# Softmax sums of a masked attention unit: in every second grouped step, products with ones on TensorE in place of VectorE's transposing reduction

## The chip, the cores and the metric

One NeuronCore of a Trainium2 chip runs the kernel. TensorE multiplies matrices and writes to PSUM, which has 8 banks of 128 partitions by 512 fp32 numbers; VectorE, ScalarE and GpSimd are three more engines with instruction queues of their own, each worked off in order; SyncE issues DMA transfers. The metric is the device time of one execution in microseconds, as the median of several. Before the change it is 3578.74 us (three runs, 3578.55 to 3579.28).

## The reference

Four cross attentions follow one another, each with a residual, for a batch of 4 sequences of 512 rows and 256 columns against a context of 1024 rows and 512 columns. Layers 0, 2 and 3 are alike and called masked here; layer 1 is called grouped. All arithmetic is fp32. Cut to what matters:

```python
# layers 0, 2, 3 ("masked"): 16 heads of 64
q, k, v = x @ Wq, ctx @ Wk, ctx @ Wv
logits = q @ k.T / 8 + col_bias            # col_bias: -20 * (1 - mask) in at most four key columns
probs  = softmax(logits, axis=keys)        # over 1024 keys
x      = probs @ v @ Wo + bo + x
# layer 1 ("grouped"): 16 query heads of 16, 4 key heads of 16
xn    = x * rsqrt(mean(x * x) + eps) * norm_w
probs = softmax((xn @ wq) @ (ctx @ wk).T / 4)
x     = x + probs @ (ctx @ wv) @ wo
```

The part of it that the change touches is the sum over keys by which the exponentials of a masked layer are divided.

## The kernel before

**Tiling.** Everything is kept transposed: logits have the keys on partitions and the queries along the free axis. A *unit* of a masked layer is a pair of heads of one sequence: 8 tiles of 128 keys (on partitions) by 1024 columns, which are 512 queries of the one head and 512 of the other. A unit of the grouped layer is a quarter of its heads in two halves, `h` 0 and 1, again 8 tiles of 128 by 1024 each. There are 96 masked units and 32 grouped ones. One *step* works on one masked unit, and in 32 of the 96 on a grouped unit too; `order()` lays the units out by two strings of digits (`MASKED_TURNS`, `GROUPED_TURNS`), so that grouped units with `h` 0 and 1 fall on alternate steps. A product of fp32 matrices of 512 columns appears in the profile as two records.

**A masked unit.** In its own step, `scores` (L803, L809) makes the 8 logit tiles, ScalarE copies each to SBUF (L813), and VectorE keeps a running maximum (L817). `max_quarters` and `max_everywhere` reduce that maximum over partitions and spread it again (L854 to L880). VectorE subtracts it from each tile (L888), ScalarE takes the exponential (L894), and GpSimd adds the 8 exponential tiles up into one, `g.acc` (L933, seven additions). In the *next* step the unit is called `g1`: `attend` multiplies the exponentials with the values on TensorE (L833) into `g1.place`, a PSUM bank, and `normalise(g1)` works on VectorE: `reciprocal_sums` reduces `g.acc` over partitions with a transposing reduction (L854 reading `st`), adds the quarters up in small pieces (L958 to L963), takes the reciprocal (L966), spreads it by a transposition (L968), and `scale_out` multiplies the attended values by it (L979), which gives the bank of `g1.place` back. One PSUM bank serves `reciprocal_sums` as room. `project_out` (L997) takes the result through Wo a step or more later, two units at a time.

**A grouped unit** (`lam`). Its logits are made one step ahead, as `coming`, by four calls of `logits_pair` (L780), which take two double PSUM banks each and give one or both of them back when ScalarE has copied them (L786). In its own step GpSimd subtracts the maximum (L886), ScalarE takes the exponentials, `attend_grouped` multiplies with the values (L833, 32 columns wide), and `keep_even` (ScalarE, L843) and `keep_odd` (VectorE, L847) bring the halves of the result to SBUF. After the second half, `h` = 1, `turn_grouped` divides by the sum, which a column of ones in the values has made: VectorE instructions L944, L945, L946 and L950, with one PSUM bank as room.

**What sets the order.** The schedule is written out by hand in the step loop. TensorE's work between the scores and the next step is a list, `fill`, of (estimated us, function). In a step with a grouped unit of `h` = 1 it is: the output projection of two units (3.6), the projection of one or two query sets (1.7 each, L721), and the eight parts of the keys of the next two units (1.7 each, L514; two parts, `part` 0 and 1, accumulate in one bank). `attend_grouped` (3.6) is inserted where the estimates ahead of it reach 9.5:

```python
            while where < len(fill) and total < 9.5:
                total += fill[where][0]
                where += 1
            fill.insert(where, (3.6, attend_grouped))
```

As the list is gone through, a running estimate `now` decides when `events` (the subtractions and exponentials of the unit) are issued to VectorE and ScalarE, and when the four `logits_pair` calls come in between, the first at 12.0. Ahead of the first one, `behind_exponentials` issues the rest of `events` and then the list `late`: `normalise(g1)`, `keep_odd(lam)` and, where `h` = 1, `turn_grouped(lam)`, in this order on VectorE.

**PSUM banks.** `Place(width)` hands out banks at the time of building, the one given back longest ago first (a single bank whose neighbour is taken is preferred); what a bank's next user waits for on the chip follows from that choice. In the 16 steps with `h` = 1 there are three kinds. In ten the list has two query projections; in two (the second halves of the first quarter in sequences 1 and of the second quarter in sequence 3) it has one; in both kinds the four pairs of the next grouped unit follow. In four steps (each sequence's last) it has at most one and there is no next grouped unit, so no pairs.

Of the kernel before, what the change touches and what calls it, by code (L numbers as in the profile page):

```python
# [16 lines left out]
P = 128  # L17
B, S, C = 4, 512, 256
# [62 lines left out]
def kernel(ctx: ExitStack, tc: tile.TileContext, a: dict, out: bass.AP):  # L81
    nc = tc.nc
# [8 lines left out]
    def t_(shape, tag, name, bufs=1, dtype=FP):  # L91
        return sb.tile(shape, dtype, tag=tag, name=name, bufs=bufs)
# [40 lines left out]
    def give_set(g):  # L133
        sets_free.append(g.set)
# [6 lines left out]
    ones = t_([P, P], "ones", "ones")  # L141
# [595 lines left out]
    def reciprocal_rows(out_, in_, room):  # L737


        turned = room[:, 0:S]  # L740
        short = t_([P, S // 32, 1], "short", f"short{len(turns)}")
        turns.append(0)
        nc.vector.transpose(turned, in_)
        nc.vector.reciprocal(short, turned.rearrange("p (c r) -> p c r", r=32)[:, :, 0:1])
        nc.vector.transpose(
            out_.rearrange("p (c r) -> p c r", r=32), short.to_broadcast([P, S // 32, 32])
        )
# [71 lines left out]
    def place_out(g, width=1):  # L819
        g.place = Place(width)  # L820
        g.po, g.psum = g.place.ap[:, 0:S], g.place.ap[:, S:]

    def attend(g, blocks=range(NT)):
        for t in blocks:
            for j in range(2):
                rows = g.rows[j]
                if not g.masked:
                    rows = slice(64 * g.h + 32 * j, 64 * g.h + 32 * (j + 1))
                at, first, last = rows, 0, NT - 1
                if not g.masked:  # L830
                    at = slice(64 * (t % 2) + 32 * j, 64 * (t % 2) + 32 * (j + 1))
                    first, last = t % 2, NT - 2 + t % 2
                nc.tensor.matmul(  # L833
                    g.po[at, :], lhsT=g.v[:, t, rows], rhs=g.st[t][:, j * S : (j + 1) * S],
                    start=(t == first), stop=(t == last),
                )

    def keep_even(g):


        if g.h == 0:
            gq[g.b, "o"] = t_([P, S], "o1", f"o1_{g.name}")
        nc.scalar.copy(gq[g.b, "o"][64 * g.h : 64 * (g.h + 1), :], g.po[0:64, :])  # L843

    def keep_odd(g):
        half = gq[g.b, "o"][64 * g.h : 64 * (g.h + 1), :]
        nc.vector.tensor_tensor(half, half, g.po[64:128, :], ALU.add)  # L847
        g.place.back()
# [35 lines left out]
    def subtract(g, t):  # L884
        if not g.masked:
            nc.gpsimd.tensor_tensor(g.st[t], g.st[t], g.mb, ALU.subtract)  # L886
            return
        nc.vector.tensor_tensor(g.st[t], g.st[t], g.mb, ALU.subtract)  # L888
        if t == NT - 1:
            g.mb_place.back()  # L890
# [18 lines left out]
    def attend_last(g):  # L909

        place_out(g, 2)
        parts_of = [g.st[t] for t in range(g.now, NT)] + [g.acc]

        def add(n):
            for j in range(2):
                nc.tensor.matmul(
                    g.psum[g.rows[j], :], lhsT=ones[:, 0:64], rhs=parts_of[n][:, j * S : (j + 1) * S],
                    start=(n == 0), stop=(n == NT - g.now),
                )

        for t in range(NT):
            for j in range(2):
                nc.tensor.matmul(
                    g.po[g.rows[j], :], lhsT=g.v[:, t, g.rows[j]], rhs=g.st[t][:, j * S : (j + 1) * S],
                    start=(t == 0), stop=(t == NT - 1),
                )
            if t >= g.now:
                add(t - g.now)
        add(NT - g.now)
        g.ot = t_([P, S], "ot", f"ot_{g.name}", bufs=3)  # L930
# [4 lines left out]
    def turn_grouped(g):  # L935
        w = Place(1)
        normalise_grouped(g, w.ap)
        w.back()
# [33 lines left out]
    def normalise(g):  # L972
        w = Place(1)
        reciprocal_sums(g, w.ap)
        w.back()
        scale_out(g)

    def scale_out(g):
        nc.vector.tensor_tensor(g.ot, g.po, g.ot, ALU.mult)  # L979
        g.place.back()  # L980

    def project_out(*of):

        g = of[0]
        x, acc = xs[g.l, g.b], xs.get((g.l + 1, g.b))
        opens = acc is None
        if opens and g.masked:
            acc = new_state(g.l + 1, g.b)
        elif opens:

            acc = xs[g.l + 1, g.b] = x
            x_at[g.l + 1, g.b] = x_at[g.l, g.b]
        w = Place()
        m = w.ap
        for k in range(KC):
            for each in of:
                nc.tensor.matmul(  # L997
                    m[:, k * S : (k + 1) * S], lhsT=each.wo[:, k * P : (k + 1) * P], rhs=each.ot,
                    start=each is g, stop=each is of[-1],
                )  # L1000
        y = m.rearrange("p (k q) -> p k q", q=S)

        def add_last(q):
            nc.vector.tensor_tensor(acc[:, :, q], y[:, :, q], acc[:, :, q], ALU.add)

        def add():
            if g is masked[-1]:
                for i in range(0, NI, 2):
                    add_last(slice(i * P, (i + 2) * P))
                    store(g.b, range(i, i + 2))  # L1010
                left[g.b] = -1
            elif opens and g.masked:
                bo = columns[f"L{g.l}_xattn_bo"]
                for k in range(KC):
                    nc.vector.scalar_tensor_tensor(
                        acc[:, k, :], y[:, k, :], bo[:, k : k + 1], x[:, k, :], ALU.add, ALU.add
                    )
            else:
                nc.vector.tensor_tensor(acc, y, x if opens else acc, ALU.add)
            w.back()  # L1020

        left[g.b] -= len(of)
        return add
# [33 lines left out]
    def at(n):  # L1057
        return steps[n] if 0 <= n < len(steps) else (None, None)
# [8 lines left out]
    def head(g):  # L1067
        return steps[step_of[1, g.b, 0]][1]
# [28 lines left out]
    g0, g1 = masked[0:2]  # L1097
# [41 lines left out]
    for n in range(len(steps) + 2):  # L1139
        g, lam = at(n)  # L1140
        follows, coming = at(n + 1)
        soon = at(n + 2)[1]
        g1, attended = attended, g
        ending = n >= len(steps) - 2
# [61 lines left out]
        late = []  # L1206
# [23 lines left out]
        for each in (follows, coming):  # L1230
            if each and (not (each.l and each.u == 0) if each.masked else each.h == 0):
                queries.append(each)

        if lam:
            for t in range(NT):
                subtract(lam, t)
# [11 lines left out]
        if g1 and g:  # L1248
            attend(g1)
            give_set(g1)  # L1250
            if not ending:
                late.append(lambda: normalise(g1))
        elif g1:
            attend_last(g1)
            adds = [project_out(*each) for each in outs]
            outs = []
            reciprocal_rows(g1.ot, g1.psum, g1.mx)
            scale_out(g1)
            for add in adds:
                add()  # L1260
# [8 lines left out]
        if coming:  # L1269
# [6 lines left out]
        fill, of_grouped = (  # L1276
            [
                (1.8 * len(each), lambda each=each: project_out(*each))
                for each in outs if each[0].masked == m
            ]  # L1280
            for m in (True, False)
        )
        outs = []
        of_queries = [(1.7, lambda each=each: project_q(each)) for each in queries]
        if fast_k:
# [3 lines left out]
            fill = of_keys[:2] + fill + of_keys[2:4] + of_queries + of_keys[4:]  # L1289
        elif fast_v:  # L1290
            of_values = fast_values(g)
            fill = of_values[:2] + fill + of_queries + of_values[2:]
# [6 lines left out]
        if lam:  # L1299

            def attend_grouped():
                while any(of is lam for _, of, _ in events):
                    events.pop(0)[2]()
                lam.v = head(lam).v
                place_out(lam)
                attend(lam)
                give_set(lam)
                late.append(lambda: keep_odd(lam))
                if lam.h == 1:
                    late.append(lambda: turn_grouped(lam))  # L1310
                return lambda: keep_even(lam)

            total, where = 0.0, 0
            while where < len(fill) and total < 9.5:
                total += fill[where][0]
                where += 1
            fill.insert(where, (3.6, attend_grouped))
# [17 lines left out]
        if g1 and g and ending:  # L1335

            def by_products():
                sums(g1)
                return lambda: late.append(
                    lambda: (reciprocal_rows(g1.ot, g1.psum, g1.mx), scale_out(g1))  # L1340
                )

            fill.append((0.9, by_products))
# [48 lines left out]
```

## Time and profile before

| | |
|---|---|
| runs | 3578.55, 3578.74, 3579.28 us |
| profiled execution | 3578.93 us, of which the span of its instructions is 3577.2 us; mean granted TensorE clock 0.995 |
| TensorE | 3495.1 us of matrix products, 98% of the span |
| VectorE | 3045.3 us, 85% |
| GpSimd | 2495.9 us, 70% |
| ScalarE | 2352.9 us, 66% |
| steps with a grouped unit of `h` = 1 | ten of 49.64 to 51.28 us, two of 52.59 and 53.39 us, four of 39.07 to 40.13 us |
| L854 reading `st` (VectorE) | 1257 ns, 93 times |
| L958, L959, L960, L963 (four), L966, L968, L979 (VectorE) | 193, 191, 181, 165 each, 253, 711, 692 ns |
| L833, 64 columns wide (TensorE) | 32 records, that is 16 products, in 7.02 us |

Times are microseconds from the first instruction unless marked ns. PE is TensorE, PEld its weight loads, DVE VectorE, ACT ScalarE, POOL GpSimd. A line of the timeline has the start, the length from the first start to the last end, engine, source line, operation, what is written and read, sizes, and how many; in square brackets stands how long the engine had been idle and who ended that. The ends of matrix products are modelled, so lengths of a stage on TensorE are better taken from one start to the next. The granted clock is a share of full speed. The length of a step is the time from its first L803 to the next step's.

### The profile page before, as it was taken

Reading aid. Unit: us, or ns where it says so; the run is one execution under the profiler, and the core shown is the slowest. Engines: PE = TensorE matmul, PEld = TensorE weight load, DVE = VectorE, ACT = ScalarE, POOL = GpSimd, SP = SyncE. Lnnn points to the kernel's source line nnn. Section 1 sums busy time; section 2 is a strip of 40 time slices with the busy share of each in tenths; the row PEclk is TensorE's granted clock in tenths of the full one; section 3 lists DMA queues with packets and bytes.
Section 4 is the critical chain, followed back from the end, with each engine's and each line's share of the span. In section 5 each row is a group of like instructions: output and inputs, shape, how many; then the busy total and the mean of one; then the engine's idle time right before and its main releaser. Section 6 shows DMA issues by size and latency. Waiting matters only on the chain.

```text
span 3577.2 us, 42743 instructions
## 1 busy us (share of the span) xinstructions
PE 3495.1 (98%) x15390; PEld 1703.6 (48%) x15390; DVE 3045.3 (85%) x4174; ACT 2352.9 (66%) x2737; POOL 2495.9 (70%) x1273
## 2 busy tenths in 40 slices
PE   8999999999999999999999999999999999999998
PEld 4454444444444444444554545454444445454554
DVE  7878788987889978889888888888788988888887
ACT  4565577775777757777565666665577775666664
POOL 3565477774777747777678778777477776769774
PEclk9999999999999999999999999999999999999999
DMA  3222101002100020001001111010201011002110
GB/s 90 62 93 82 56 20 46 23 19 56 39 23 23 19 78 17 23 23 43 27 27 50 33 33 51 27 51 18 57 22 38 23 34 43 26 27 74 33 32 7
DMA packets 159384, 140.16 MB, mean 39 GB/s; under 512 B 42424, under 2 KB 142264, under 8 KB 158660
## 3 DMA queue, kind: packets, MB, share of 16 engines
q1 hardware_dynamic: 153518, 124.32, 11.2%
q0 software_dynamic: 2560, 8.39, 0.7%
q10 hardware_dynamic: 3094, 4.72, 0.6%
q8 instruction: 122, 2.00, 0.2%
q14 instruction: 90, 0.74, 0.1%
HBM read 122.71 MB, written 10.49 MB: 37 GB/s over the span
## 4 chain that ended last, share of the span: by engine, by line
PE 67%; DVE 23%; ACT 7%; issue 3%; POOL 1%; ACTq 0%; DMA 0%; DVEq 0%; SPq 0%; POOLq 0%
PE ps L608 13%; PE ps L803 13%; PE ps L833 13%; PE ps L514 9%; DVE ps L817 8%; PE ps L553 7%; DVE st L888 5%; ACT st L894 4%; PE ps L780 3%; PE ps L721 3%; PE ps L997 3%; DVE ps L854 2%; DVE ps L880 1%; DVE ps L792 1%; ACT st L786 1%
## 5 line engine op out<-in xcount | busy, mean ns | idle before, releaser
L933 POOL TENSOR_TENSOR st<-st 128x1024 f32<-128x1024 f32 x668 | 1581.0, 2367 | 725.6 <-ACT st L894 680.8
L894 ACT ACTIVATE st<-st 128x1024 f32<-128x1024 f32 x1024 | 1036.3, 1058 | 300.1 <-DVE st L888 233.6
L817 DVE TENSOR_TENSOR ps<-ps,st 128x1024 f32<-128x1024 f32 x672 | 828.0, 1232 | 295.7 <-ACT st L813 234.2
L888 DVE TENSOR_TENSOR st<-st,ps 128x1024 f32<-128x1024 f32 x768 | 883.5, 1216 | 3.3
L886 POOL TENSOR_TENSOR st<-st 128x1024 f32<-128x1024 f32 x256 | 596.8, 2374 | 312.4 <-DVE st L880 207.0
L833 PE MATMUL ps<-st,v 128*64 128x512 f32 (+1 forms) x4064 | 800.7, 595 | 9.0 <-ACT st L894 8.9
L813 ACT COPY st<-ps 128x1024 f32<-128x1024 f32 x768 | 716.6, 1048 | 96.5 <-PE ps L809 65.1
L803 PE MATMUL ps<-qt,kt 64*128 64x512 f32 x3072 | 719.5, 601 | 26.4 <-DVE ps L854 19.6
L833 PEld LDWEIGHTS ps<-st,v 128*64 128x64 f32 (+1 forms) x4064 | 241.4, 130 | 550.2 <-issue 435.5
L803 PEld LDWEIGHTS ps<-qt,kt 64*128 64x128 f32 x3072 | 301.9, 186 | 382.4 <-issue 131.3
L514 PE MATMUL ps<-ctx,wk 128*128 128x512 f32 x896 | 417.1, 611 | 2.2 <-ACT ctx L416 1.1
L553 PE MATMUL ps<-wv,ctx 128*128 128x256 f32 x1792 | 408.0, 382 | 0.0
L553 PEld LDWEIGHTS ps<-wv,ctx 128*128 128x128 f32 x1792 | 335.5, 190 | 102.4 <-issue 59.4
L792 DVE TENSOR_TENSOR ps<-ps,st 128x1024 f32<-128x1024 f32 x224 | 276.1, 1232 | 73.3 <-ACT st L786 60.2
L786 ACT COPY st<-ps 128x1024 f32<-128x1024 f32 x256 | 247.4, 1014 | 83.1 <-PE ps L780 80.2
L514 PEld LDWEIGHTS ps<-ctx,wk 128*128 128x128 f32 x896 | 167.3, 193 | 239.5 <-issue 215.5
L608 PE MATMUL ps<-st 128*128 128x128 f32 (+1 forms) x1200 | 229.0, 339 | 6.4 <-ACT ps L631 6.4
L623 ACT COPY st<-ps 128x512 f32<-128x512 f32 x40 | 23.4, 585 | 301.6 <-PE ps L608 301.6
L780 PE MATMUL ps<-qt,kt 32*128 32x512 f32 x1024 | 183.3, 640 | 18.0 <-DVE o L847 9.7
L608 PEld LDWEIGHTS ps<-st 128*128 128x128 f32 x1200 | 158.6, 192 | 75.1 <-issue 65.1
L721 PE MATMUL ps<-x,wq 128*128 128x512 f32 x384 | 186.2, 608 | 1.3 <-ACT x L379 1.1
L997 PE MATMUL ps<-ot,wo 128*128 128x512 f32 x384 | 175.8, 600 | 0.7 <-DVE ot L979 0.7
(177 smaller groups left out, 2833.1 us busy)
## 6 DMA issues: line engine op xcount, KB each, us to landing
ctx<-kept SPq DMA_DIRECT2D x24, 1024.0 KB
wk<-in_L_xattn_Wk_dram SPq DMA_DIRECT2D x47, 512.0 KB
wv<-in_L_xattn_Wv_dram SPq DMA_DIRECT2D x47, 512.0 KB
wq<-in_L_xattn_Wq_dram SPq DMA_DIRECT2D x96, 128.0 KB
wo<-in_L_xattn_Wo_dram SPq DMA_DIRECT2D x96, 128.0 KB
st<-kept SPq DMA_DIRECT2D x4, 2048.0 KB
kept<-st SPq DMA_DIRECT2D x12, 512.0 KB
qt<-qt ACTq DMA_DIRECT2D x32, 128.0 KB
```

Of the source, the lines that this page charges most:

```text
L514: nc.tensor.matmul(m, lhsT=g.w["k"][:, k, :], rhs=ctx_half[g.b, n][:, k, :], start=(k == 0), stop=(k == KT - 1),)
L553: nc.tensor.matmul(m[:, half * 2 * P : (half + 1) * 2 * P], lhsT=ctx_half[g.b, t // 4][:, k, t % 4 * P : (t % 4 + 1) * P], rhs=g.w["v2"][: ...
L608: nc.tensor.matmul(m if is_keys else m[:, q], lhsT=right[:, k, :] if is_keys else left_[:, k, q], rhs=left_[:, k, :] if is_keys else right ...
L792: nc.vector.tensor_tensor(top, top, g.st[t], ALU.max)
L803: nc.tensor.matmul(m[:, j * S : (j + 1) * S], lhsT=g.kt[g.rows[j], keys], rhs=g.qt[g.rows[j], :], start=True, stop=t > 0,)
L813: nc.scalar.copy(g.st[t], m)
L817: nc.vector.tensor_tensor(top, top, g.st[t], ALU.max)
L833: nc.tensor.matmul(g.po[at, :], lhsT=g.v[:, t, rows], rhs=g.st[t][:, j * S : (j + 1) * S], start=(t == first), stop=(t == last),)
L886: nc.gpsimd.tensor_tensor(g.st[t], g.st[t], g.mb, ALU.subtract)
L888: nc.vector.tensor_tensor(g.st[t], g.st[t], g.mb, ALU.subtract)
L894: nc.scalar.activation(st, st, AF.Exp)
L933: nc.gpsimd.tensor_tensor(g.acc, g.st[0] if t == 1 else g.acc, g.st[t], ALU.add)
```

## The change

In steps whose grouped unit has `h` = 1 (and that have both `g` and `g1`), `normalise(g1)` is not put on `late`. In its place a new item goes into `fill` behind the first one, with an estimate of 0.9: `sums_beside(g1)` takes a PSUM bank and issues two products of a 128 by 64 matrix of ones with the two halves of `g1.acc` on TensorE, which leave in every row of the bank the sums of the head that this row belongs to. It then puts `turned` at the front of `late`: VectorE transposes that bank into `g.ot` (L743), takes the reciprocal of one column in 32 (L744), spreads it by a second transposition (L745, which are the lines of `reciprocal_rows`), gives the bank back and does `scale_out`. The estimate of 0.9 counts in the loop that places `attend_grouped`, and in `now`.

```diff
+    def sums_beside(g):
+        w = Place(1)
+        for j in range(2):
+            nc.tensor.matmul(
+                w.ap[g.rows[j], :], lhsT=ones[:, 0:64], rhs=g.acc[:, j * S : (j + 1) * S],
+                start=True, stop=True,
+            )
+
+        def turned():
+            g.ot = t_([P, S], "ot", f"ot_{g.name}", bufs=3)
+            reciprocal_rows(g.ot, w.ap, g.ot)
+            w.back()
+            scale_out(g)
+
+        return turned
...
+        by_ones = bool(g and g1 and lam and lam.h == 1)
...
-            if not ending:
+            if not ending and not by_ones:
                 late.append(lambda: normalise(g1))
...
+            if by_ones:
+                fill.insert(1, (0.9, lambda: late.insert(0, sums_beside(g1))))
             total, where = 0.0, 0
             while where < len(fill) and total < 9.5:
```

Built, the two programs differ in the 16 steps with `h` = 1 in three ways beside the instructions exchanged:

- On TensorE `attend_grouped` stands one key part (L514, two products) earlier, and that part follows the fourth pair; without pairs it simply follows `attend_grouped`.
- On ScalarE, in the ten steps with two query projections, the grouped unit's eighth exponential keeps its place behind the same work, and the first copy of keys (L519) moves from ahead of L843 to behind the first pair's copies. In the two steps with one query projection the eighth exponential moves from behind the first L519 to ahead of it.
- PSUM banks are dealt out differently. In the ten steps the first pair's second double bank is now the one that holds `g1.place` and the sums, where it was one of a freed query bank and a freed key bank; the second pair's first double bank now holds the room of `turn_grouped`, where it was the banks of `g1.place` and of the grouped unit. In the two steps the first pair's second double bank was that of `g1.place` and of the grouped unit and is now one of freed query and key banks; the second pair's first one holds the room of `turn_grouped` in both programs.

The order in the other steps is unchanged. Lines from L979 on have numbers higher by 16 to 19 in the changed kernel.

## The prediction

> **What bounds the kernel now.** I read the page first: busy times, then the chain that ended last.
>
> ```profile
> PE 3495.1 (98%) x15390; PEld 1703.6 (48%) x15390; DVE 3045.3 (85%) x4174; ACT 2352.9 (66%) x2737; POOL 2495.9 (70%) x1273
> PE 67%; DVE 23%; ACT 7%; issue 3%; POOL 1%; ACTq 0%; DMA 0%; DVEq 0%; SPq 0%; POOLq 0%
> ```
>
> TensorE is nearly always in use, so a product added costs its time unless it falls into a wait of TensorE, and VectorE time taken away gains only where TensorE waits for it. Next the waits of TensorE over the whole run:
>
> ```profile
> PE ps L803 <- DVE ps L854: 19.6, 16, 1.8
> PE ps L780 <- DVE o L847: 9.7, 14, 1.1
> PE ps L833 <- ACT st L894: 8.9, 10, 1.2
> ```
>
> The columns after the colon are total us, times, longest. The first is in the scores, ahead of the change. The others are the attention and the pairs of grouped steps, so I read the timeline of one changed step (it starts at 583.52 and lasts 49.64 us), TensorE first, then ScalarE and VectorE:
>
> ```profile
> 603.24 1.88 PE L721 MATMUL ps<-x,wq 128*128 128x512 f32 x4
> ...
> 606.67 3.60 PE L514 MATMUL ps<-ctx,wk 128*128 128x512 f32 x8
> 610.20 3.63 PE L833 MATMUL ps<-st,v 128*32 128x512 f32 x28
> 614.61 1.05 PE L833 MATMUL ps<-st,v 128*32 128x512 f32 x4 [0.79 <-ACT st L894]
> 615.60 1.70 PE L780 MATMUL ps<-qt,kt 32*128 32x512 f32 x8
> 617.22 1.98 PE L514 MATMUL ps<-ctx,wk 128*128 128x512 f32 x4
> 619.14 2.62 PE L780 MATMUL ps<-qt,kt 32*128 32x512 f32 x8
> 621.68 1.98 PE L514 MATMUL ps<-ctx,wk 128*128 128x512 f32 x4
> ```
>
> ScalarE:
>
> ```profile
> 612.56 2.95 ACT L894 ACTIVATE st<-st 128x1024 f32<-128x1024 f32 x3 [0.55 <-DVE st L888]
> 615.53 0.58 ACT L519 COPY kt<-ps 128x512 f32<-128x512 f32 x1
> 616.01 2.01 ACT L894 ACTIVATE st<-st 128x1024 f32<-128x1024 f32 x2
> 618.05 0.58 ACT L843 COPY o<-ps 64x512 f32<-64x512 f32 x1
> ```
>
> VectorE:
>
> ```profile
> 613.06 1.26 DVE L854 TRANSPOSE_TENSOR_REDUCE ps<-st 128x32 f32<-128x1024 f32 x1
> ...
> 618.66 0.69 DVE L847 TENSOR_TENSOR o<-o,ps 64x512 f32<-64x512 f32 x1 [1.18 <-ACT o L843]
> ...
> 621.20 0.69 DVE L950 TENSOR_TENSOR o<-o,ps 128x512 f32<-128x512 f32 x1
> ```
>
> See three things. The last block of the grouped attention starts at 614.61, when its exponential (the second of the three at 612.56) ends; TensorE has been out of work since about 610.20 + 28 x 0.1115 = 613.32 (0.1115 is a record of the undisturbed attention, 32 in 3.57 us, in the step that starts at 633.16). A pair takes 1.07 us undisturbed (the third, from 623.60 to 624.67); the first takes 1.62 and the second 2.54, so they wait 0.55 and 1.47 us. And behind the chain that the change shortens VectorE stands idle for 1.18 us until ScalarE's L843. So VectorE's work there isn't on the path now.
>
> **The change part by part.** *VectorE.* Removed per step: 1257 + 193 + 191 + 181 + 4 x 165 + 253 + 711 ns, 3.45 us. Added: two transpositions and a reciprocal, 716 + 253 + 712 ns by the same lines at the kernel's end, 1.68. Its queue is 1.8 us shorter, but L847, the next on it, waits for L843: worth nothing by itself.
>
> *TensorE.* The two products are four records at 7.02 / 32 = 0.22, 0.88 us a step. Their sums have been ready since GpSimd's last addition at 580.3, 23 us before 603.2, so they add no wait there. That GpSimd's subtractions come next on its queue changes nothing.
>
> *The attention one key part earlier.* In ten steps (like this one) TensorE now arrives at 603.24 + 0.88 + 3.43 (L721) + 1.77 (one key part) = 609.32 in place of 610.20. The eighth exponential has the same work ahead of it on ScalarE, which was in arrears, so it ends at the same time and the last block starts at 614.61 as before. The products hide in that wait, and 0.88 us more of it is idle, but a key part of 1.77 us is left for later. (That key part's bank is now one of the projection's, which VectorE's L1019 frees at 607.49, while TensorE comes at 607.55; what it might lose there falls into the wait too.)
>
> *The first pair* begins at 615.60. Its second half waited for the copy L519, which is done at 616.11. It will use the banks of the sums and of the attended values, which VectorE frees at 613.06 + 0.75 + 0.29 + 0.75 + 0.69 = 615.54 (the rows with their pauses): no wait, and it ends at 616.67 rather than 617.22. The key part behind it ends at 618.59.
>
> *The second pair* is the dear one. It must now wait for the end of `turn_grouped`, L950. L843 starts 0.6 us earlier, as L519 no longer stands ahead of it, so L847 runs from about 618.06, and L950 ends 3.23 us later (618.66 to 621.89 now): 621.29. The pair runs from 621.35 to 622.42, where it was done at 621.68: 0.74 us later, after an idle time of 2.8 us. What is queued behind the waiting pair is all of TensorE's work, two more pairs and the keys.
>
> *The rest of the step* took 11.48 us and has 1.77 more, less the 0.16 that the fourth pair waited. Sum for such a step: 0.74 + 1.77 - 0.1 = 2.4 us. The next step starts later by as much, and its engines begin with what its scores bring, so nothing is made up.
>
> *Two steps* (at 938 and 2721) have one query projection. In the latter, counted from its start, the eighth exponential comes about 0.6 us sooner on ScalarE, as a copy of keys no longer precedes it, so the last block starts at 30.65 rather than 31.25 and the first pair, whose banks are free, runs from 31.63 to 32.70; a key part ends at 34.6. L843 stays behind all exponentials, so L950 still ends at 37.9 and the second pair runs from 37.95 to 39.0. Behind it come 1.92 + 1.07 + 1.92 + 1.07 + 3.53 + 1.72 + 1.81: the step ends at 52.05 in place of 52.59, -0.5 us. I take that for both. *Four steps* have no pairs and hardly wait in the attention (32 records in 3.61 us): 0.88 each. Sum: 10 x 2.4 - 2 x 0.5 + 4 x 0.88 = 26.5 us.
>
> *The clock.* What 26.5 leaves out is in this table of stretches in the step at 2721, whose pairs wait long already (length, busy times of the five engines, granted clock, DMA):
>
> ```profile
> 2753.60:2757.00 3.40, 2.47 (x8) 0.58 (x4) 2.63 (x4) 2.96 (x4) 3.32 (x2) 1.00 0.00 0
> 2757.00:2760.40 3.40, 3.40 (x6) 1.18 (x4) 2.96 (x5) 1.01 (x1) 3.24 (x3) 0.51 0.00 0
> ```
>
> After a stretch in which products were few, the clock is halved for 3.4 us, though all that time is busy; its L514 records stand 0.85 us apart in place of 0.43. That costs 1.7 us. Five stretches more are like it (near 429, 876, 975, 1392, 2634; each has a mean of 0.66 over 5 us), all behind about 1.5 to 2.5 us of idle time within some 3.5. The ten steps, with waits of 1.3 and 1.5 us that lie apart, have none. The changed step has two waits, of 2.2 us in the attention and 2.8 at the second pair. A drop after the first is nearly hidden by the second; one after the second costs 1.7 us in full. Bounds: none in any step, 0 us; one in each of the twelve, 12 x 1.7 = 20.4. I take half of the ten and both of the others, as their wait at the second pair grows to 3.3 us, at 1.5 each since part of the 3.4 us may still lie in the wait: 7 x 1.5 = 10.5. Sum 37 us.
>
> [...]
>
> The profiled execution took 3578.93 us, its span and 1.7, against a median of 3578.74: both give 3616 with 37 added.
>
> **The rivals.**
> *No drop of the clock:* all of the above without 10.5. Speaks for it: no drop in the ten steps now. Against: the longer waits. 3578.7 + 26.5 = 3605.
> *A drop in every step with pairs:* 26.5 + 20.4 gives 3626.
> *Not slower: the second pair doesn't wait for L950.* The place is the bank that the pair takes. Were it free, the pair would start on arrival at 618.59, 2.8 us earlier, and a step of the ten would end 0.3 us sooner than now; with 3.5 for the four and -1 for the two that is 3578, no change. It decides at a wait under 0.4 us. Against it: the profile shows pairs of the step at 2721 held by L979 and L847 through their banks, and L950 stands on the same queue behind them.
> *A gain from VectorE's 1.8 us:* it would need VectorE, not ScalarE's L843, to be late for the pairs; the 1.18 us idle ahead of L847 says no. At most the second pair's 1.47 us in ten steps less 3.5: 3567.
> *The sums wait for GpSimd:* each us would cost ten to sixteen; 23 us of margin speak against it.
>
> **How the numbers follow.** Forecast 3616 (some drops) 0.45; no drop, 3605, 0.25; drops everywhere, 3626 or somewhat above, 0.18; mis-sized second wait between 3587 and 3600, 0.05; not slower 0.05; gain 0.02. The range runs from the no-drop case less 6 us to the all-drops case with 4 more: 3599 to 3630. A measurement of this kernel tells about 0.2% (7 us) from no change: slower 0.93, same 0.05, faster 0.02.
>
> **What would show it.** In the changed kernel: four new records near 20 us into each of the 16 steps without idle time ahead; the last attention block still about 31.1 us in; a second pair that starts near 37.8 us and waits for L950; ten steps near 52.0 us, or 53.7 with a stretch at half clock; four near 39.95. It is wrong if ScalarE's exponentials move, if the pairs' banks are freed sooner than I have it, or if the next step makes the time up.

## The result, and the profile after

The changed kernel takes 3619.24 us (median of four runs, 3618.18 to 3621.81) against 3579.01 for the kernel before beside it (3578.55 to 3579.94): a ratio of 1.0114 with a 95% interval of 1.0101 to 1.0126, slower by 40 us. The profiled execution took 3619.03 us, its span is 3617.3 us and its mean granted clock 0.992.

The page after, busy times and the chain that ended last:

```profile
PE 3504.4 (97%) x15454; PEld 1697.4 (47%) x15454; DVE 3017.1 (83%) x4062; ACT 2350.3 (65%) x2737; POOL 2495.3 (69%) x1273
PE 67%; DVE 23%; ACT 6%; issue 2%; ACTq 0%; DVEq 0%; DMA 0%; POOL 0%; POOLq 0%
```

VectorE has lost 28 us of work and TensorE has gained 9, which explains neither the direction nor the size. The waits of TensorE over the whole run do (total us, times, longest):

```profile
PE ps L780 <- DVE o L950: 29.2, 12, 2.7
PE ps L803 <- DVE ps L854: 19.2, 16, 1.8
PE ps L833 <- ACT st L894: 13.4, 11, 1.3
PE ps L780 <- DVE o L847: 9.2, 14, 0.7
```

The first line is new: a pair of the coming grouped unit waits for L950, the end of the turn in place, once in each of the twelve steps that have pairs. The scores' wait (second line) is as before, the grouped attention's (third) went from 8.9 to 13.4 us.

The step that the prediction followed now starts at 585.77. Its timeline, TensorE:

```profile
605.59 1.08 PE L981 MATMUL ps<-st,ones 128*64 128x512 f32 x4
606.60 1.98 PE L721 MATMUL ps<-x,wq 128*128 128x512 f32 x4
...
610.13 1.88 PE L514 MATMUL ps<-ctx,wk 128*128 128x512 f32 x4
611.94 3.63 PE L833 MATMUL ps<-st,v 128*32 128x512 f32 x28
616.88 1.05 PE L833 MATMUL ps<-st,v 128*32 128x512 f32 x4 [1.31 <-ACT st L894]
617.86 1.14 PE L780 MATMUL ps<-qt,kt 32*128 32x512 f32 x8
618.93 1.98 PE L514 MATMUL ps<-ctx,wk 128*128 128x512 f32 x4
623.59 2.09 PE L780 MATMUL ps<-qt,kt 32*128 32x512 f32 x8 [2.67 <-DVE o L950]
625.61 2.56 PE L514 MATMUL ps<-ctx,wk 128*128 128x512 f32 x4
```

VectorE in the same step:

```profile
620.30 0.69 DVE L847 TENSOR_TENSOR o<-o,ps 64x512 f32<-64x512 f32 x1 [2.52 <-ACT o L843]
...
622.85 0.69 DVE L950 TENSOR_TENSOR o<-o,ps 128x512 f32<-128x512 f32 x1
```

Read it from the top. The two products start at 605.59, with no idle time ahead of them. The attention comes 1.77 us of work earlier and finds the eighth exponential unfinished, so its last block starts at 616.88, 31.11 us into the step, where it also started before. The first pair no longer waits. The second one does, for 2.67 us, until L950 is done. VectorE's queue is shorter by 1.8 us, and most of that is now idle time ahead of L847 (2.52 us until ScalarE's L843, where it was 1.18). The pair and the key part behind it are then slow (2.02 us to the next start in place of 1.07, a length of 2.56 in place of 1.98). The stretches around them show why (from and to, length, busy times of the five engines with the number of instructions, granted clock, DMA):

```profile
616.56:619.97 3.41, 3.09 (x15) 1.01 (x16) 1.19 (x2) 3.38 (x5) 3.33 (x2) 1.00 0.01 2
619.97:623.39 3.42, 0.95 (x3) 0.12 (x1) 2.95 (x5) 2.72 (x4) 3.26 (x3) 1.00 0.00 0
623.39:626.80 3.41, 3.21 (x10) 1.19 (x11) 1.33 (x3) 1.09 (x2) 3.33 (x2) 0.50 0.00 0
```

In the second stretch TensorE was busy for 0.95 us of 3.42; in the third it has half clock. Such a stretch at half clock is called a drop here.

Step by step, from one first L803 to the next: the ten steps with two query projections are 2.43 us longer where the clock did not drop (three of them) and 3.6 to 4.2 us longer where it did (seven). Together that is 35.2 us. The two steps with one projection together add 0.9, the four without pairs 4.6, and all other steps take back 0.5. The sum is 40.1 us, the difference of the two profiled executions.

### The profile page after: what moved, and what is told of

It reads as the page before. It is cut to its first block, busy times and chain, and to the rows that moved or that the text cites. A ratio compares the mean times of both kernels' runs of the same rounds, so it can differ in the third digit from the quotient of the medians.

```text
span 3617.3 us, 42774 instructions
## 1 busy us (share of the span) xinstructions
PE 3504.4 (97%) x15454; PEld 1697.4 (47%) x15454; DVE 3017.1 (83%) x4062; ACT 2350.3 (65%) x2737; POOL 2495.3 (69%) x1273
## 4 chain that ended last, share of the span: by engine, by line
PE 67%; DVE 23%; ACT 6%; issue 2%; ACTq 0%; DVEq 0%; DMA 0%; POOL 0%; POOLq 0%
PE ps L608 13%; PE ps L803 13%; PE ps L833 12%; PE ps L514 9%; DVE ps L817 8%; PE ps L553 7%; DVE st L888 5%; ACT st L894 4%; PE ps L780 4%; PE ps L721 3%; PE ps L1013 3%; DVE ps L854 2%; DVE ps L880 1%; DVE ps L792 1%; DVE every L869 1%
## 5 line engine op out<-in xcount | busy, mean ns | idle before, releaser
L833 PE MATMUL ps<-st,v 128*64 128x512 f32 (+1 forms) x4064 | 802.2, 595 | 14.1 <-ACT st L894 13.4
L803 PE MATMUL ps<-qt,kt 64*128 64x512 f32 x3072 | 716.6, 599 | 25.3 <-DVE ps L854 19.2
L803 PEld LDWEIGHTS ps<-qt,kt 64*128 64x128 f32 x3072 | 298.4, 186 | 381.4 <-ACT st L813 134.2
L514 PE MATMUL ps<-ctx,wk 128*128 128x512 f32 x896 | 424.1, 619 | 2.2 <-ACT ctx L416 2.2
L792 DVE TENSOR_TENSOR ps<-ps,st 128x1024 f32<-128x1024 f32 x224 | 276.1, 1233 | 97.2 <-ACT st L786 86.8
L514 PEld LDWEIGHTS ps<-ctx,wk 128*128 128x128 f32 x896 | 169.3, 196 | 245.3 <-issue 225.3
L780 PE MATMUL ps<-qt,kt 32*128 32x512 f32 x1024 | 167.2, 654 | 44.3 <-DVE o L950 29.2
L721 PE MATMUL ps<-x,wq 128*128 128x512 f32 x384 | 187.5, 611 | 1.7 <-ACT x L379 1.1
L1013 PE MATMUL ps<-ot,wo 128*128 128x512 f32 x384 | 175.8, 600 | 0.7 <-DVE ot L995 0.7
```

The source lines that it names most:

```text
L514: nc.tensor.matmul(m, lhsT=g.w["k"][:, k, :], rhs=ctx_half[g.b, n][:, k, :], start=(k == 0), stop=(k == KT - 1),)
L792: nc.vector.tensor_tensor(top, top, g.st[t], ALU.max)
L803: nc.tensor.matmul(m[:, j * S : (j + 1) * S], lhsT=g.kt[g.rows[j], keys], rhs=g.qt[g.rows[j], :], start=True, stop=t > 0,)
L833: nc.tensor.matmul(g.po[at, :], lhsT=g.v[:, t, rows], rhs=g.st[t][:, j * S : (j + 1) * S], start=(t == first), stop=(t == last),)
```

## The experiments

Each ran beside the kernel before on the same chip. The columns "ten", "two", "four" and "rest" give by how many us the steps of each kind, together, were longer in the profiled execution than in that of before; "rest" is all other steps and the ends.

| run | median us | ratio to before, 95% interval | ten | two | four | rest |
|---|---|---|---|---|---|---|
| changed kernel | 3619.2 | 1.0114 [1.0101, 1.0126] | +35.2 | +0.9 | +4.6 | -0.5 |
| attention at its old place | 3588.0 | 1.0025 [1.0015, 1.0035] | +6.1 | +0.5 | +4.4 | -1.7 |
| early place alone | 3637.7 | 1.0163 [1.0149, 1.0177] | +48.8 | +2.3 | +5.0 | +2.4 |
| products alone | 3589.5 | 1.0027 [1.0017, 1.0038] | +7.0 | +1.6 | +6.2 | -1.4 |
| VectorE's path alone | 3576.4 | 0.9991 [0.9982, 1.0000] | +0.2 | +2.9 | -0.3 | -3.1 |
| wait filled, two products | 3606.3 | 1.0073 [1.0060, 1.0087] | +23.7 | -0.8 | +4.6 | +0.3 |
| wait filled, one product | 3606.7 | 1.0078 [1.0064, 1.0091] | +23.7 | -0.8 | +4.6 | +0.2 |
| room given back late | 3611.4 | 1.0085 [1.0071, 1.0099] | +20.4 | +2.7 | +4.6 | +4.7 |
| attention one part later | 3607.8 | 1.0079 [1.0065, 1.0093] | -3.9 | -4.4 | +4.1 | +32.1 |
| put together | 3579.3 | 1.0000 [0.9991, 1.0009] | -0.7 | -4.9 | 0.0 | +5.9 |
| put together, second | 3573.6 | 0.9983 [0.9974, 0.9992] | +1.6 | -4.5 | -0.3 | -1.8 |
| before, room late | 3581.0 | 1.0005 [0.9996, 1.0014] | 0.0 | -0.3 | 0.0 | +0.6 |

The theory: the loss comes from the place of the attention, which the 0.9 in the list moves one key part ahead. That leaves the key part for later, deals out the banks so that the second pair waits for L950, and the wait brings the clock down. The rivals: the products cost their own time, VectorE's new path delays something, or the clock drops for another reason.

### Attention at its old place

```diff
-                fill.insert(1, (0.9, lambda: late.insert(0, sums_beside(g1))))
+                fill.insert(1, (0.0, lambda: late.insert(0, sums_beside(g1))))
```

> The changed kernel, with the estimate of the sums in the list of fillers set from 0.9 to 0.0, so that the grouped attention stays behind as many key parts as before; the products and VectorE's shorter path stay. Theory (the loss is the attention's place: the key part left for later and, through the banks, the second pair's wait for L950): in the ten steps the second pair takes a double bank without the turn's room, so they return to within 0.3 us of the kernel before, the products hidden in the attention's wait; the four steps without pairs keep their +0.9 to +1.25 us, of which most comes back in the step behind; no more than one or two drops of the clock beyond the six of before. Time 3579 to 3586, that is 33 to 40 us under the changed kernel. Rival (the products themselves cost about 1.2 us in each of 16 steps): about 3598.

Measured: 3588.0 us, 31 us under the changed kernel and 2 above the range given. The ten steps are back: five are within 0.02 us of before and one 0.45 shorter. Four have a drop and are 1.5 to 1.7 us longer. The wait for L950 is left in the two steps alone:

```profile
PE ps L803 <- DVE ps L854: 19.2, 16, 1.8
PE ps L780 <- DVE o L847: 8.9, 12, 0.7
...
PE ps L780 <- DVE o L950: 5.3, 2, 2.7
```

The theory holds, and the products, which are all in this kernel, cost nothing in the ten steps. The estimate also counts in `now`, so the edit takes back, with the place, the new order on ScalarE (L519 stands ahead of L843 again); the two were not tried apart. What was missed is the four drops there. TensorE in this kernel, the step that starts at 583.21:

```profile
611.10 4.27 PE L833 MATMUL ps<-st,v 128*32 128x512 f32 x32
615.30 1.14 PE L780 MATMUL ps<-qt,kt 32*128 32x512 f32 x8
616.37 1.98 PE L514 MATMUL ps<-ctx,wk 128*128 128x512 f32 x4
618.29 3.17 PE L780 MATMUL ps<-qt,kt 32*128 32x512 f32 x8
```

The first pair runs in 1.07 us, since VectorE's shorter path has freed its banks (with the products and the long path, in the third experiment, it waits 0.80 us in such a step for that path's end). The time that it saves comes back inside the second pair, which takes 3.10 us to the next start where 1.07 is its own: one wait of 2.0 us where there were two of 0.55 and 1.47.

### The early place alone

```diff
             total, where = 0.0, 0
+            if g and g1 and lam.h == 1:
+                fill.insert(1, (0.9, lambda: None))
```

This is an edit of the kernel before.

> The kernel before, with only an empty filler of 0.9 us put where the changed kernel has its sums, so that the grouped attention stands one key part earlier; no products, normalise as before. Theory (the place makes the loss): a key part of 1.77 us is left for later and the first pair now needs the bank that L847 frees, so that the second pair comes some 0.7 us later as well: the ten steps are 1.8 to 2.6 us longer, the four unchanged, with some drops of the clock on top: 3597 to 3617. Rival (the products or VectorE's order make it): 3579, within 3 us.

Measured: 3637.7 us, 58 above before and 18 above the changed kernel. So the place makes the loss without any product, and more of it than I had worked out. The waits name what I missed:

```profile
PE ps L833 <- ACT st L894: 29.5, 17, 2.7
...
PE ps L780 <- DVE o L847: 9.2, 12, 1.1
PE ps L780 <- DVE ot L979: 8.8, 11, 1.3
```

The attention waits 29.5 us for its exponentials, as no product fills the time, and the first pair waits for L979, the end of VectorE's long path. TensorE in one of its steps without a drop (686.23):

```profile
711.28 3.63 PE L833 MATMUL ps<-st,v 128*32 128x512 f32 x28
717.34 1.05 PE L833 MATMUL ps<-st,v 128*32 128x512 f32 x4 [2.43 <-ACT st L894]
718.33 1.13 PE L780 MATMUL ps<-qt,kt 32*128 32x512 f32 x4
720.25 2.38 PE L780 MATMUL ps<-qt,kt 32*128 32x512 f32 x4 [0.80 <-DVE ot L979]
```

That step is 2.89 us longer than before, others 4.1 to 6.6 with drops. No pair waits for L950 in this kernel: the early place makes a loss by itself, but through other waits than in the changed kernel, where it is the second pair's wait for L950. The products and VectorE's shorter path therefore repay 18 us of what the early place costs. Which of the two repays how much at that place wasn't tried.

### The products alone

The kernel before, with `sums_beside` called from a filler of 0.0; its bank is given back at once and `normalise` stays:

```diff
+                fill.insert(1, (0.0, lambda: sums_beside(g1)))
```

> The kernel before with only the products added: their sums go to a bank that is given back at once and nobody reads them, VectorE turns and adds as before, and the attention keeps its place. Theory: in the ten steps the products fall into the attention's wait of 1.3 us and cost under 0.2 us; the four steps without pairs are 0.9 to 1.25 us longer, of which 0.7 comes back in the next; time 3579 to 3585. Rival (a product always costs its time, TensorE being 98% busy): 16 x 1.0 to 1.2, about 3597.

Measured: 3589.5 us, above the range given. The reading by steps is clear all the same: five of the ten are within 0.01 us of before, so the products are hidden there. The rest of the ten's 7.0 us lies in five steps with drops (1.1 to 1.7 each; one of the five, which starts at 1386.55 in the kernel before, has a drop in its scores there too). In three of the four steps without pairs 1.92 us were added and 0.74 came back in the step behind. The rival's 16 x 1.0 to 1.2 is out; that drops would appear was not foreseen.

### VectorE's path alone

```diff
-        w = Place(1)
-        for j in range(2):
-            nc.tensor.matmul(
-                w.ap[g.rows[j], :], lhsT=ones[:, 0:64], rhs=g.acc[:, j * S : (j + 1) * S],
-                start=True, stop=True,
-            )
...
-            reciprocal_rows(g.ot, w.ap, g.ot)
-            w.back()
+            reciprocal_rows(g.ot, g.po, g.ot)
```

These are edits of the changed kernel, and the estimate is 0.0 as in the first experiment, so that the attention is at its old place. The kernel leaves out the sums by which the output is divided.

> The kernel before with VectorE's shorter path alone: two transpositions and a reciprocal, taken of the attended values that stand in their bank already, in place of the nine operations on the sums; no products, so what the output is divided by is left out. The attention keeps its place. Theory: at the old place VectorE stands idle ahead of L847 until ScalarE's L843, so its 1.8 us a step are worth nothing: 3576 to 3582. Rival (VectorE's queue holds the pairs): up to 1.5 us in each of ten steps, 3564 to 3570.

Measured: 3576.4 us, in the theory's range; the ten steps differ by 0.2 us in all. VectorE's 1.8 us are worth nothing there, and the rival's 10 us or more are out.

### The wait filled

```diff
+    def fill_wait(m, rhs):                  # called in the key part behind the first pair
+        for _ in range(idle[0]):
+            nc.tensor.matmul(m, lhsT=zeros, rhs=rhs, start=False, stop=False)
...
+            idle[0] = 2 if i == 0 and by_ones else 0
```

> The changed kernel with two more products per step with pairs (weights of zeros added to the sum that a key part builds up, so it stays the same), right behind the first pair, in the time that TensorE waits for L950: 2 x 0.86 us of the 2.7. Theory (the drops to half clock come from that idle time): the ten steps stay 2.4 us longer than before, for the wait only gets shorter, but lose most of their seven drops: 3606 to 3612, some 7 to 13 us under the changed kernel, although it computes more. Rival (the drops have another cause, or come anyway): 3618 to 3622; if the products delay anything behind them, more.

Measured: 3606.3 us, 13 us faster than the changed kernel with 24 products more. TensorE in the step that starts at 585.98 (in this kernel lines from L514 on stand 10 to 12 higher, so L792 is L780 and L962 is L950):

```profile
618.08 1.14 PE L792 MATMUL ps<-qt,kt 32*128 32x512 f32 x8
619.15 1.98 PE L508 MATMUL ps<-ctx,zeros 128*128 128x512 f32 x4
620.98 1.88 PE L524 MATMUL ps<-ctx,wk 128*128 128x512 f32 x4
623.81 1.14 PE L792 MATMUL ps<-qt,kt 32*128 32x512 f32 x8 [0.95 <-DVE o L962]
```

The second pair starts as late as before, 37.83 us into its step, but at full clock. The ten steps are 1.97 to 2.44 us longer than in the kernel before, and none has a drop. The steps that had drops in the changed kernel, seven of the ten and the one at 2721 of before, are each 1.5 to 1.75 us shorter now, 13.2 us together. That is what the drops had cost, and the idle time of TensorE in this wait was their cause.

### The wait half filled

```diff
-            idle[0] = 2 if i == 0 and by_ones else 0
+            idle[0] = 1 if i == 0 and by_ones else 0
```

> The changed kernel with one product with zeros behind the first pair in place of two. The wait for L950 then has 2.67 - 0.86 = 1.8 us of idle time. In the runs so far every drop begins at a whole number of 3.4133 us from every other of its run, and follows a stretch of that grid with little product work. Theory (a drop needs about 2 us of idle time within one such stretch): few drops in the twelve, none to four, the ten steps 2.4 us longer than before otherwise: 3606 to 3613. Rival (any long wait brings it): seven drops or more, 3617 to 3621.

Measured: 3606.7 us, no drop in the twelve steps. The second pair of the step that starts at 585.78, in the timeline of TensorE:

```profile
623.60 1.14 PE L792 MATMUL ps<-qt,kt 32*128 32x512 f32 x8 [1.81 <-DVE o L962]
```

So 1.81 us of idle time brought no drop, although it leaves TensorE busy for only 1.60 of the 3.41 us from 620.48 to 623.89 (columns as in the stretches of the result):

```profile
620.48:623.89 3.41, 1.60 (x8) 0.54 (x10) 3.27 (x6) 2.24 (x3) 3.33 (x2) 1.00 0.00 0
623.89:627.30 3.41, 3.41 (x20) 1.16 (x15) 2.18 (x3) 1.93 (x2) 3.33 (x2) 1.00 0.00 0
```

One needless product a step does as much as two.

### The room of the turn given back late

```diff
     def turn_grouped(g):
...
-        w.back()
+        w.back(6)
```

> The changed kernel, attention at its early place, with one edit: the bank of the turn in place counts as given back six returns later, so that the second pair's first product takes the double bank that the first pair's second half had, which ScalarE's L786 has copied out some 1.3 us before L950 ends. Theory (the second pair waits for L950 through its bank, and the drops come from that wait): the second pair starts 1.2 to 1.3 us sooner in all twelve steps, the wait shrinks to about 1.4 us, and nearly all drops of the twelve go: 12 x 1.25 + 8 x 1.5 = 27 us under the changed kernel, 3588 to 3598; the ten steps stay about 1.2 us longer than before. Rival (the pair would wait as long for something else, or L950 is only what the trace names): 3616 to 3622.

Measured: 3611.4 us, 8 under the changed kernel where 21 to 31 were expected, but not the rival's 3616 or more. TensorE's waits, and the pairs in the step that starts at 584.49:

```profile
PE ps L780 <- ACT st L786: 16.1, 12, 1.4
```

```profile
616.59 1.14 PE L780 MATMUL ps<-qt,kt 32*128 32x512 f32 x8
617.66 1.98 PE L514 MATMUL ps<-ctx,wk 128*128 128x512 f32 x4
621.00 1.62 PE L780 MATMUL ps<-qt,kt 32*128 32x512 f32 x8 [1.36 <-ACT st L786]
```

The wait for L950 is gone and the pair starts 1.31 us sooner in its step (36.51 in place of 37.82), as the theory has it. The pair itself then takes 1.54 us to the next start in place of 1.07, so 0.84 us of the gain is left in each of the steps without a drop. Five of the twelve still have one, three of the ten and both of the two. And the late room deals out the banks of the four steps differently too, which costs 1.8 us in the step behind each (+1.05 in three where the changed kernel has -0.74).

### The attention one part later

```diff
-                fill.insert(1, (0.9, lambda: late.insert(0, sums_beside(g1))))
+                fill.insert(1, (0.0, lambda: late.insert(0, sums_beside(g1))))
             total, where = 0.0, 0
-            while where < len(fill) and total < 9.5:
+            while where < len(fill) and total < (10.5 if lam.h == 1 else 9.5):
```

> The changed kernel with the estimate of the sums at 0.0 and the attention's threshold at 10.5 in place of 9.5 in these steps, which puts it one key part later than in the kernel before, behind the first pair. Theory (the attention's place is what counts, and it comes too early): the wait for L894 is gone, 0.8 to 1.3 us in ten steps, and at most the wait inside the second pair on top: 3567 to 3582. Rival (L843, L847 and the pairs behind them move along, so a new wait takes the old one's place): 3588, as with the old place, or up to 20 us more.

Measured: 3607.8 us. Seven of the ten steps are shorter, by 0.5 to 1.3 us, as the theory had it, but the twelve steps behind those with pairs are 34 us longer together: the rival's new wait, in another step. The gain in one step can thus be read only with the step behind it. The waits of TensorE:

```profile
PE ps L803 <- DVE o L950: 17.7, 12, 1.5
PE ps L833 <- ACT kt L519: 17.0, 10, 1.8
```

The attention comes later, and with it L847 and L950; what stands behind them are now the scores of the next step.

### Put together, and the kernel before with the late room

The first of two: attention at its old place, products only in the twelve steps with pairs, the late room, one product with zeros behind the first pair.

```diff
-        by_ones = bool(g and g1 and lam and lam.h == 1)
+        by_ones = bool(g and g1 and lam and lam.h == 1 and coming)
...
-                fill.insert(1, (0.9, lambda: late.insert(0, sums_beside(g1))))
+                fill.insert(1, (0.0, lambda: late.insert(0, sums_beside(g1))))
...
-        w.back()
+        w.back(6)
```

> What the runs so far point to, put together: the changed kernel with the estimate of the sums at 0.0 (attention at its old place), the products only in the twelve steps that have pairs, the turn's room given back six returns later, and one product with zeros behind the first pair to keep idle time short. Theory: the ten steps are as long as in the kernel before, the steps at 938 and 2721 lose 1.3 us of their wait for L950 and their drop (1.5) each, the four are unchanged: 3570 to 3576, under both kernels by at least 0.1%. Rival (the zeros' product delays the second pair by its 0.86 us, or drops come elsewhere): 3579 to 3590.

Measured: 3579.3 us, the time of the kernel before, so the rival's range. The two steps lost 4.9 us (5.6 were expected), but the steps behind the four became 4 x 1.79 = 7.2 longer, the late room's price. The second gives the room back late in the twelve steps only:

```diff
-                    late.append(lambda: turn_grouped(lam))
+                    late.append(lambda: turn_grouped(lam, 6 if coming else 0))
```

> The kernel of the run before this one (attention at its old place, products only in the twelve steps with pairs, one product with zeros behind the first pair), with the turn's room given back late only in those twelve steps, since in the four others the late room cost 1.79 us each in the step behind. Theory: the steps at 938 and 2721 keep their 4.9 us together, the 4 x 1.79 go: 3579.3 less about 7, 3570 to 3575. Rival (the four steps' cost comes from elsewhere, or drops move): 3577 to 3581.

Measured: 3573.6 us, ratio 0.9983 [0.9974, 0.9992], the fastest of all: 6.5 us under the kernel before, 46 under the changed one. The interval excludes 1, though 0.17% is about as little as can be told. In the profiled executions 4.5 us of it lie in the two steps; the other groups, among which drops have come and gone, nearly cancel out.

The third is the kernel before with the late room in the twelve steps and nothing else:

```diff
-        w.back()
+        w.back(late)
...
-                    late.append(lambda: turn_grouped(lam))
+                    late.append(lambda: turn_grouped(lam, 6 if coming else 0))
```

> The kernel before with one edit: the turn's room counts as given back six returns later in the twelve steps with pairs; no products. Theory (what the run before gains lies in the two steps whose second pair waits for L950, and has nothing to do with the products): those two steps lose 1.3 us of wait and a drop of 1.5 each, the ten others stay as they are: 3572 to 3576, like the one beside it. Rival (the products or VectorE's shorter path are what gains): 3578 to 3581.

Measured: 3581.0 us, no gain: the rival. Its timeline in the step that starts at 2722.11 shows why the room alone doesn't do it:

```profile
2754.34 1.13 PE L780 MATMUL ps<-qt,kt 32*128 32x512 f32 x4
2756.13 1.12 PE L780 MATMUL ps<-qt,kt 32*128 32x512 f32 x2 [0.67 <-DVE ot L979]
2757.52 1.12 PE L780 MATMUL ps<-qt,kt 32*128 32x512 f32 x2 [0.27 <-DVE o L847]
```

Once the pairs take other banks, the first one stands behind L979, the end of VectorE's long path, and L847. So in these two steps neither part gains alone: the room without VectorE's shorter path gives -0.3 us, the shorter path with the products but without the room (the first experiment) +0.5, that path without products +2.9, room and path together, with the product of zeros, -4.5. What the product of zeros adds to that wasn't tried apart.

## Why the prediction was right

The forecast was 3616 us with a range of 3599 to 3630; 3619.2 was measured. Its steps against the runs:

| step of the prediction | forecast | measured |
|---|---|---|
| last attention block after the step's start | 31.1 us | 31.11 |
| second pair waits for L950, starts at | 37.8 us | 37.82, a wait of 2.67 |
| one of the ten without a drop | 52.0 us, +2.4 | 52.08, +2.43 |
| ten without drops | +24 | +23.7 (with the wait filled) |
| two without drops | -1.0 | -0.8 (with the wait filled) |
| four without pairs | +3.5 | +4.6; the steps behind three of them 0.74 shorter each, the one behind the fourth 0.9 longer |
| drops of the clock in the twelve | 7 x 1.5 = 10.5 | 8, 13.2 together |

*The attention one key part earlier* and *the second pair* were right in place and, in the ten, in size: the wait is for L950, on all twelve steps. In the two, the pair was done when forecast, but its wait for L950 is 1.42 us and not 3.3: the first pair, whose banks were to be free, takes 1.63 us in place of 1.07, and two records of the second pair go ahead of the wait. The experiment that undoes the place alone gave 31 of the 40 us back, and filling the wait gave the clock's share, 13, alone.

*VectorE's 1.8 us are worth nothing* holds at the old place, where that path alone changed the ten steps by 0.2 us. It is true of the changed kernel only because the new path is there. With the long path at the early place, the first pair would have waited for L979, and that kernel takes 3637.7 us. The prediction used this without saying so: the sentence that the first pair's banks are free at 615.54 counts with the short path.

*The products* are hidden in the ten, as said. In the four steps they were sized at 0.88 us and cost 1.25 in three. Started one after the other they take 1.01 us, and the products ahead of and behind them are 0.1 us longer to the next start (3.63 for 3.54 of the output projection, L1013 here and L997 before, and in the ten steps 3.53 for 3.43 of the two L721). Nothing was counted for the steps behind these; 0.74 us came back behind three of them and 0.90 was added behind the fourth.

*The clock* is the term that was mis-sized. The forecast was half of the ten and both of the others; it was seven of the ten and one of the two, at 1.65 us rather than 1.5. That half of the ten came as near as it did is partly luck, as the prediction had nothing that tells one step from another; the last section shows how the ten differ. In the 3.41 us ahead of the six drops of before TensorE is idle for 0.9 to 2.1 us by the rows (the line shown has 2.47 us busy of 3.40), less than the 1.5 to 2.5 that it read within some 3.5. And two of the six, at 1391.74 and 2634.19, lie in the scores of two of the ten steps, so that "the ten steps have none" is true of their pairs alone. The longest wait of the ten in the changed kernel is 2.67 us, and seven of them dropped.

*Not slower* was to decide at a second wait under 0.4 us; it was 2.67. *The sums wait for GpSimd*: they start without idle time.

## What to carry to other kernels

An estimate in a scheduling list is part of the change: here 0.9 us of estimate for work that fell into a wait anyway moved a neighbour by 1.8 us and dealt out the banks anew, and undoing it gave 31 of the 40 us back. When an engine is 98% busy, look up what each of its waits is for before a product is called dear or an engine's relief is called a gain; the products cost nothing in ten steps and VectorE's relief brought nothing. A wait of TensorE may cost more afterwards through the clock: here waits of 1.4 to 2.7 us did in eight of twelve steps, 1.65 us each on average, and a needless product put into it gave that back.

## What the runs showed of the hardware

I had not expected that the drops of the clock lie at regular distances. In the profiled executions of the kernel before and of the changed one, each begins a whole number of 3.4133 us from every other of its run, to within 0.02 us: in the kernel before, 2757.07 - 975.32 = 1781.75 = 522.0 x 3.4133; in the changed one, 718.97 - 623.39 = 95.58 = 28.0 x 3.4133. Such a row of times 3.4133 us apart is called a grid here. Between start-up and end the six drops of before and ten of the eleven of the changed kernel last 3.41 us; the one at 886.22 lasts 6.83. In the two kernels it lies differently against the same work: the drop near 429 begins 30.55 us into its step in the kernel before and 30.33 in the changed one.

How a wait lies on the grid differs between steps. Two steps of the changed kernel have the same wait of 2.67 us. In the one at 585.77, above, 2.47 us of idle time fall into one stretch, and the next is at half clock. In the one at 490.66 the wait, from 526.57 to 529.24, is cut by the grid:

```profile
524.40:527.81 3.41, 2.17 (x8) 0.68 (x4) 1.75 (x4) 3.36 (x5) 3.33 (x2) 1.00 0.00 0
527.81:531.23 3.42, 1.99 (x10) 0.80 (x11) 2.48 (x3) 1.37 (x3) 3.26 (x3) 1.00 0.00 0
```

There is idle time of 1.24 and 1.43 us on either side of 527.81 and full clock in both. In the ten steps of the changed kernel this goes with the drops in all cases: the largest part of the wait within one stretch is 1.43 to 1.55 us in the three without a drop there and 1.82 to 2.67 us in the seven with one.

Idle time alone doesn't settle it, though. Where the wait was half filled, 1.81 us brought no drop in the step shown above, while 1.42 us, from 2791.67 to 2793.09, did in the changed kernel's step at 2755 (half clock from 2794.27 on, TensorE busy for 2.00 of the 3.42 us ahead). With the attention at its old place half clock even follows a stretch in which TensorE is shown busy for 3.31 of 3.41 us:

```profile
708.99:712.40 3.41, 3.31 (x9) 0.89 (x8) 2.85 (x5) 3.32 (x4) 3.33 (x2) 1.00 0.00 0
712.40:715.81 3.41, 3.41 (x6) 1.17 (x4) 3.20 (x4) 1.01 (x1) 3.33 (x2) 0.50 0.02 5
```

That stretch holds the eight records of one pair, of 32 rows each, which take 3.17 us from the first start to the last end, where undisturbed it is 1.14. What else than idle time sets off a drop was not shown.

My guess is that this is also why small edits are followed by gains and losses of 1 to 3 us in steps whose work they don't lengthen, as a shift of the rest of the program moves other waits to another place on the grid; it was not tried apart. In the kernel with the products alone, for instance, the ten steps are equal to before within 0.01 us in five cases and up to 1.7 us longer in the others.
